# Turning taps and h2 on TensorE: 128-row transposes, or two of 64 rows in two banks of PSUM

## The chip, the cores and the metric

The kernel runs on one core of one Trainium2 chip (trn2). The metric is the device time of one execution in microseconds; the median of several runs is compared. All of the arithmetic is in 32-bit floats.

## The reference, cut to what matters

The input x has 4 images, 256 channels and 64 x 64 pixels. Two layers follow each other. The first works out, for each pixel, 49 attention weights (a 7 x 7 window with dilation 2) and sums the shifted inputs with them. The second is a bottleneck block with batch norms whose statistics come from the data.

```python
# layer 0
k = conv(x, w1 (128,256,7,7), pad 6, rhs_dilation 2) + b1
k = conv1x1(k, w2 (49,128)) + b2
attn = softmax(k, axis=1)                       # 49 weights for each pixel
x = einsum('bkchw,bkhw->bchw', shifts, attn)    # 49 shifted copies of x
# layer 1
residual = x
h = relu(bn(conv1x1(x, w1 (64,256))))
h = relu(bn(conv3x3(h, w2 (64,64))))
h = bn(conv1x1(h, w3 (256,64)))
return relu(h + residual)
```

`bn` is a batch norm over images and pixels: it takes mean and variance of its input, and applies gamma and beta.

## The kernel before, in words

One function, `conv_seq_kernel`, holds all stages. The stages follow each other in time like this.

**Logits (0 to about 475 us).** The two convolutions of layer 0 are merged into one of 49 outputs, and computed with a transform of the rows at nine points. `column_convs` (L251, its matmul is L262) multiplies column by column of the transformed input by the transformed weights and accumulates the 49 logits of the 4 strips of columns (s = 0 to 3), two accumulators each, in the eight banks of PSUM (`accall`, a tile of 8 banks). VectorE does the transforms and combinations, all through `stt` (L151).

**Softmax and the attention matrix.** The logits of a pixel lie along the free dimension, with pixels (rows of the image, blocks of images) on the partitions. `exponents(s)` (L520) subtracts the maximum and takes the exponential on ScalarE (L527), `shares(s)` (L529) divides by the sum and puts the 7 x 7 taps with gaps into one of three row buffers `pads` (L540), so that a window of 128 columns, at the right offset, is a diagonal band. `turn(s, h)` (L555) transposes those windows on TensorE (L566), which gives the band matrices that the gather needs. For each of the four row phases j it makes 8 transposes of 128 x 128 (two windows k, four columns w) into one pair of banks of `accall`; four pairs are used in rotation, by the counter `n_turn`. The only exception is turn(0, 0), which uses the first pair for all its j. The lower 64 of the 128 partitions hold images 0 and 2 (g = 0), the upper 64 hold images 1 and 3 (g = 1). So two copies bring each group into `amat`: g = 0 and g = 1. ScalarE makes both (L573), but where `shared` is set, VectorE makes that of g = 1 (L571). turn(0, 0) runs within the last column products, in an order that the framework's scheduler chooses. The seven others (L679 to L695) stand in a block where the order of VectorE, TensorE, ScalarE and SyncE is the order of the code: (0,1), (1,0), (1,1), (2,0), and then with `shared` (2,1), (3,0), (3,1). `zero_edges` (L651, its memset is L657) clears border blocks of `amat` on GpSimd.

**Gather and first 1x1 convolution (about 504 to 655 us).** `gather` (L739, matmul L752) multiplies tiles of x, pixels by channels, by blocks of `amat`. It takes all strips of columns of one image, so it needs all turns, the g = 0 half of them for the first units. The tiles of x come by DMA (`load_xt`, L113 to L119) and their shifted copies from `shift_xt` (L123 ScalarE, L124 and L125 GpSimd). `conv1` (L777, matmul L785) follows for every second unit. `keep_y` stores the result of layer 0, which is also the residual.

**3x3 convolution (about 660 to 717 us).** `direct` (L952) and `products` (L964) work in 8 single banks of a pool `pb`, and leave h2: 128 partitions (two halves of an image, a = 0 and 1, of 64 channels each), 16 blocks of 512 pixels.

**Statistics of the last convolution (about 720 to 742 us).** The moments of the third convolution follow from the second moments of h2. For each of the 16 blocks: ScalarE applies the batch norm and relu (L1024), TensorE transposes four times 128 x 128 into one bank (L1027), VectorE copies the bank into one of three buffers `ht` (L1029), in which a column of ones stands behind every 64 values, and TensorE accumulates 64 x 65 moments (L1032), for the two halves in the two column halves of the array. A float matmul takes two passes, which the trace shows as two records: 8 calls a block are 16 matmuls and 16 weight loads. A transpose is one record of each. The framework's scheduler orders this stage. `pt` comes from the pool of 8 banks, in which `moments` holds one.

**Last convolution and output (about 742 to 790 us).** `conv3` (L1009, matmul L1014) multiplies 64 rows of h2 by w3, alternately on the lower and upper 64 partitions; VectorE adds the residual (L1071), ScalarE applies the relu (L1076), SyncE stores.

Of the kernel before, what the change touches and what calls it, by code (L numbers as in the profile page):

```python
# [42 lines left out]
F32 = mybir.dt.float32  # L43
# [3 lines left out]
PSUM = bass.MemoryType.PSUM  # L47

P = 128
# [6 lines left out]
MID = 64  # L56
# [11 lines left out]
NS, WS = 4, 8  # L68
# [25 lines left out]
def conv_seq_kernel(ctx: ExitStack, tc: tile.TileContext, xp, xt, w1, b1, w2t, b2, m1t, g1, be1,  # L94
                    m2t, g2, be2, m3t, g3, be3, z, mask, pavg, out, ydram):
    nc = tc.nc
    def pool(stack, name, bufs, space=None, **kw):
        if space is not None:
            kw["space"] = space
        return stack.enter_context(tc.tile_pool(name=name, bufs=bufs, **kw))  # L100
# [143 lines left out]
    accall = pool(s_acc, "accp", 1, PSUM).tile([P, 2 * NS, 512], F32, name="acc")  # L244
# [243 lines left out]
    ident = late.tile([P, P], F32, name="ident")  # L488
# [8 lines left out]
    for g in range(2):  # L497
        half = slice(g * MID, (g + 1) * MID)
# [7 lines left out]
    outer = pool(ctx, "outerp", 1).tile([P, OUTER], F32, name="outer")  # L506
# [46 lines left out]
    n_turn = [0]  # L553

    def turn(s, h, shared=False):  # L555

        row = pads[(2 * s + h) % 3]
        for j in range(4):
            pt = accall[:, 2 * (n_turn[0] % NS) : 2 * (n_turn[0] % NS) + 2].rearrange("p a (m n) -> p (a m) n", n=P)
            if h == 0 and s == 0:  # L560
                pt = accall[:, :2].rearrange("p a (m n) -> p (a m) n", n=P)
            n_turn[0] += 1
            for k in range(2):
                for w in range(4):
                    o = 35 - (WS * s + 4 * h + w) + P * k
                    nc.tensor.transpose(pt[:, 4 * k + w, :], row[:, j, w, o : o + P], ident)  # L566
            for g in range(2):
                dst = amat[:, g, 2 * (2 * s + h) + j % 2, j // 2].rearrange("p (n k) e -> p k n e", k=2)
                src = pt[:, :, 64 * g : 64 * g + 64].rearrange("p (k w) n -> p k n w", k=2)
                if shared and g:  # L570
                    nc.vector.tensor_copy(dst, src)  # L571
                else:
                    nc.scalar.copy(dst, src)  # L573
# [49 lines left out]
    for n, (p, factor, left) in enumerate(passes):  # L623
        if n == 0:
            continue
        u = weights(n, 1)
        if p is None:
            for s in range(NS):
                visit(slots, strip(s), p, left)
            for t in pads:  # L630
                nc.gpsimd.memset(t, 0.0)
        for s in range(NS):
            if n == 2:
                apply_factor(slots, factor, NR - 2, strip(s))
            if p is not None:
                visit(slots, strip(s), p, left)
            for d in ([s] if s == 0 else []) + ([s + 1] if s + 1 < NS else []):
                put_back(n, d)
            column_convs(s, u, False)
            if p is None:  # L640
                for d in range(s - 1 if s else 0, s + 1 if s == NS - 1 else s):
                    last_outputs(d)
            elif s > 1:
                outputs(n, p, s - 2)
            if p is None and 0 < s < NS - 1:
                if s == 2:
                    turn(0, 0)
                exponents(s - 1)
                shares(s - 1)
# [12 lines left out]
    o = 4 * XT  # L662
# [3 lines left out]
    o = OUTER - NH1  # L666
# [9 lines left out]
    with tc.manual_schedule(  # L676
        engines={mybir.EngineType.DVE, mybir.EngineType.PE, mybir.EngineType.Activation, mybir.EngineType.SP}
    ):
        turn(0, 1)  # L679
        zero_edges(0)  # L680
        load_xt(xtiles[0], *units[0])
        exponents(2)
        turn(1, 0)
        exponents(3)
        shares(2)
        turn(1, 1)
        zero_edges(1)
        turn(2, 0)
        shares(3)
        load_xt(xtiles[1], *units[0], 1)  # L690
        turn(2, 1, True)
        zero_edges(2)
        turn(3, 0, True)
        turn(3, 1, True)
        zero_edges(3)  # L695
        xts[(*units[0], 0)], xts[(*units[0], 1)] = xtiles[:2]
        nc.scalar.preload_act_table(AF.Sqrt)
        more_xt(1)

    o = NH1  # L700
# [3 lines left out]
    o = 7 * C * 4  # L704
# [182 lines left out]

    sc1, sh1 = from_stats(st1, bn12[:, 0:1], bn12[:, 1:2], bank(0)[:, :3])
    s_acc.close()
    pb_ = pool(ctx, "pb", 8, PSUM)  # L890

# [102 lines left out]
    o = 4 * 2048  # L996

    HT = 8 * (MID + 1)
    ht = [outer[:, o + HT * i : o + HT * (i + 1)].rearrange("p (j g c) -> p j g c", j=4, g=2) for i in range(3)]
    o += 3 * HT  # L1000
    for t in ht:
        nc.gpsimd.memset(t[:, :, :, MID:], 1.0)
# [14 lines left out]
        return pt[:, :n]  # L1017


    moments = pb_.tile([P, 512], F32, tag="pb", name="moments")  # L1020
    blocks = [(slot, i, q) for slot in range(2) for i in range(2) for q in range(Q)]
    for n, (slot, i, q) in enumerate(blocks):
        v = h2[:, slot, q, 512 * i : 512 * (i + 1)]
        nc.scalar.activation(v, v, AF.Relu, bias=sh2, scale=sc2)  # L1024
        pt = pb_.tile([P, 512], F32, tag="pb", name="pturn2")
        for j in range(4):
            nc.tensor.transpose(pt[:, j * P : (j + 1) * P], v[:, j * P : (j + 1) * P], ident)  # L1027
        t = ht[n % 3]
        nc.vector.tensor_copy(t[:, :, :, :MID], pt.rearrange("p (j g c) -> p j g c", j=4, g=2))  # L1029
        for j in range(4):  # L1030
            for g in range(2):
                nc.tensor.matmul(  # L1032
                    moments[g * MID : (g + 1) * MID, : MID + 1],
                    t[:, j, g, :MID],
                    t[:, j, g, :],
                    start=(n == 0 and j == 0),
                    stop=(n == len(blocks) - 1 and j == 3),
                    skip_group_check=True,
                )
# [9 lines left out]
    pt = pb_.tile([P, 512], F32, tag="pb", name="pprod")  # L1049
# [3 lines left out]
    for half in range(NH):  # L1053
        c = slice(half * P, (half + 1) * P)
# [9 lines left out]
    for k, (b, i, half) in enumerate(blocks):  # L1064
        o = ops[k % 4]

        n = 256 if k in (0, len(blocks) - 1) else 512
        for lo in range(0, 512, n):
            for q in (0, 2, 1, 3):
                v = ys[b, q, i][:, half, lo : lo + n]  # L1070
# [65 lines left out]
```

## Time and profile before

| | |
|---|---|
| Runs (us) | 796.89, 794.95, 792.17; median 794.95 |
| Profiled execution (us) | 796.58 |
| Its span (us) | 794.3 |
| Mean granted clock of TensorE | 0.972 |
| L566, 256 transposes | first 463.5, last 503.6; 273 ns each from start to end |
| L573, ScalarE's 52 copies | first 464.6, last 503.9; 680 ns median |
| L571, VectorE's 12 copies | first 496.0, last 504.6; 692 ns median |
| L1027, 64 transposes | first 721.0, last 739.5 |
| L1029, 16 copies | first 722.1, last 740.2; 682 ns median |
| L1032, 256 matmuls of the moments | first 722.9, last 741.4; 222 ns median |

How to read the profile: the span is the time from the first instruction to the last, and the execution's own time is a little more than that. Times of single instructions run from start to end; instructions of one engine overlap, so the distance between starts, not the duration, tells how fast they follow each other. PE is TensorE's matmuls, PEld its weight loads, DVE is VectorE, ACT is ScalarE, POOL is GpSimd, SP is SyncE. In a line of the timeline the columns are: start, length of the merged piece, engine, line, operation, output and input with shapes, number of instructions, and in brackets the idle time ahead of it with what ended it. A shape like 128*128 in a matmul's line is rows by columns of the array that it uses. The chain is followed back from the last instruction: at each step to what released it, or to the instruction before it on its engine.

### The profile page before, as it was taken

The numbers are of one execution on the slowest core, as the hardware profiler recorded it, in microseconds if no ns is written. First come the engines' busy times: TensorE is split into PE (matmuls) and PEld (weight loads), VectorE is DVE, ScalarE is ACT, GpSimd is POOL, SyncE is SP. The second block draws the span as 40 slices with busy tenths as digits, with TensorE's granted clock in tenths as the row PEclk, the third lists the DMA queues.
The fourth block names the chain that finished last, engine by engine and source line by source line (L and its number), as shares of the span: only waits on it lengthen the run. The fifth ranks groups of instructions, "written<-read, shape, count | busy, mean of one in ns | idle before, by whom it ended". The sixth has DMA issues, their size and how long they took to land.

```text
span 794.3 us, 10929 instructions
## 1 busy us (share of the span) xinstructions
PE 725.6 (91%) x4208; PEld 585.4 (74%) x4208; DVE 574.2 (72%) x681; ACT 297.7 (37%) x594; POOL 75.3 (9%) x143
## 2 busy tenths in 40 slices
PE   0949998999999999996999999999999997996996
PEld 0838986888888888885888888988877873445642
DVE  4489989999466999899999966522232237574797
ACT  4640156111562201110101139534443437246497
POOL 3210010000000020000001202322222210000000
PEclk9979998999999999998999999999999998998998
DMA  7941089922789788220111012467776649442299
GB/s 282 381 165 41 0 281 287 376 87 94 254 298 395 242 344 305 72 62 10 51 32 42 3 57 64 144 234 227 234 253 216 221 170 386 171 145 95 82 394 371
DMA packets 59237, 150.26 MB, mean 189 GB/s; under 512 B 7346, under 2 KB 35634, under 8 KB 55090
## 3 DMA queue, kind: packets, MB, share of 16 engines
q1 hardware_dynamic: 51216, 141.11, 49.9%
q10 hardware_dynamic: 7970, 8.45, 3.0%
q8 instruction: 33, 0.54, 0.3%
q14 instruction: 18, 0.15, 0.1%
HBM read 93.81 MB, written 55.74 MB: 188 GB/s over the span
## 4 chain that ended last, share of the span: by engine, by line
PE 71%; DVE 16%; DMA 5%; ACT 4%; issue 2%; POOL 0%; SPq 0%; ACTq 0%; DVEq 0%; POOLq 0%
PE acc L262 42%; PE acc L752 12%; DVE arena L151 8%; DVE arena L1071 4%; PE acc L785 4%; PE pconv L964 3%; PE pdirect L952 3%; DMA outer<-in_xt_dram 2%; PE acc L566 2%; PE acc L325 2%; DMA w1raw<-in_w_dram 1%; PE pturn L1027 1%; ACT arena L573 1%; PE moments L1032 1%; DMA raw<-in_xp_dram 1%
## 5 line engine op out<-in xcount | busy, mean ns | idle before, releaser
L262 PE MATMUL acc<-arena 128*128 128x343 f32 (+3 forms) x2000 | 383.9, 355 | 20.7 <-DVE arena L151 20.7
L262 PEld LDWEIGHTS acc<-arena 128*128 128x128 f32 x2000 | 324.0, 193 | 79.5 <-issue 17.8
L151 DVE SCALAR_TENSOR_TENSOR arena<-arena 128x1024 f32<-128x1024 f32 (+7 forms) x192 | 290.4, 1558 | 27.8 <-PE acc L262 17.3
L752 PEld LDWEIGHTS acc<-arena,outer 128*128 128x128 f32 x1024 | 115.5, 192 | 11.4 <-issue 9.5
L752 PE MATMUL acc<-arena,outer 128*128 128x128 f32 x1024 | 118.1, 276 | 3.2 <-issue 2.2
L793 DVE BATCH_NORM_STATS2 st<-acc 128x6 f32<-128x512 f32 x16 | 11.2, 699 | 66.6 <-PE acc L785 66.4
L286 ACT COPY sv<-acc 128x392 f32<-128x392 f32 x40 | 19.1, 484 | 101.7 <-PE acc L262 93.9
L170 ACT COPY stage<-raw 128x128 f32<-128x128 f32 x128 | 43.5, 415 | 24.4 <-DMA raw<-in_xp_dram 24.0
L325 PE MATMUL acc<-powers,w1raw 128*128 128x196 f32 (+1 forms) x196 | 45.7, 397 | 6.9 <-DMA w1raw<-in_w_dram 5.6
L325 PEld LDWEIGHTS acc<-powers,w1raw 128*128 128x128 f32 x196 | 44.8, 315 | 7.5 <-DVE arena L151 5.7
L590 ACT COPY outer<-acc 128x784 f32<-128x784 f32 x8 | 6.5, 812 | 102.7 <-PE acc L262 83.3
L1014 PE MATMUL pconv<-arena,w3m 64*128 64x512 f32 (+1 forms) x144 | 42.8, 586 | 0.6 <-DVE arena L1071 0.6
L123 ACT COPY outer<-outer 64x2048 f32<-64x2048 f32 x15 | 28.4, 1895 | 36.8 <-DMA outer<-in_xt_dram 36.7
L151 DVE SCALAR_TENSOR_TENSOR outer<-outer 128x784 f32<-128x784 f32 (+2 forms) x47 | 36.9, 838 | 3.6 <-ACT outer L906 3.6
L1014 PEld LDWEIGHTS pconv<-arena,w3m 64*128 64x128 f32 x144 | 20.7, 185 | 21.9 <-DVE arena L1071 16.1
L773 DVE COPY bks<-acc 128x256 f32<-128x256 f32 x32 | 11.3, 417 | 33.8 <-PE acc L752 33.8
L1076 ACT ACTIVATE outer<-arena 128x512 f32<-128x512 f32 (+1 forms) x58 | 34.7, 695 | 1.3 <-DVE arena L849 1.1
L1071 DVE SCALAR_TENSOR_TENSOR arena<-pconv,arena 128x512 f32<-128x512 f32 (+1 forms) x58 | 34.3, 670 | 0.0
L124 POOL COPY outer<-outer 64x1792 f32<-64x1792 f32 x15 | 25.1, 1675 | 92.8 <-DMA outer<-in_xt_dram 79.8
L607 ACT COPY acc<-bks 128x392 f32<-128x392 f32 x40 | 18.5, 488 | 40.6 <-DVE outer L592 33.8
L573 ACT COPY arena<-acc 128x512 f32<-128x512 f32 x52 | 27.1, 716 | 14.8 <-PE acc L566 14.4
L964 PE MATMUL pconv<-outer,arena 128*128 128x512 f32 x72 | 31.1, 592 | 0.0
(143 smaller groups left out, 611.2 us busy)
## 6 DMA issues: line engine op xcount, KB each, us to landing
raw<-in_xp_dram SPq DMA_DIRECT2D x36, 608.0 KB, 5.4
outer<-in_xt_dram SPq DMA_DIRECT2D x17, 896.0 KB, 6.1
out_dram<-outer SPq DMA_DIRECT2D x14, 1024.0 KB, 4.5
arena<-y_dram SPq DMA_DIRECT2D x25, 512.0 KB, 7.5
fsort_dram<-stage SPq DMA_DIRECT2D x2, 4864.0 KB, 14.8
arena<-fsort_dram SPq DMA_DIRECT2D x8, 1216.0 KB, 9.8
y_dram<-outer SPq DMA_DIRECT2D x16, 512.0 KB, 5.4
aside_dram<-sv ACTq DMA_DIRECT2D x40, 196.0 KB, 5.7
```

What stands on the lines that cost most here:

```text
L123: nc.scalar.copy(t[:MID], x[MID:])
L151: nc.vector.scalar_tensor_tensor(out, in0, scalar, in1, ALU.mult, ALU.add)
L170: (last if last and k + a == 2 else nc.scalar.copy)(d[:, k, :, PLACE[b], 2 * a : 2 * a + 2, i : i + count], raw[:, lo : lo + 4 * count - 3 ...
L262: nc.tensor.matmul(acc[i][d][:, o : o + (hi - lo) * K], xi[:, i, CW * w : CW * w + CW, :].rearrange("p x t -> p (x t)"), u[i][:, lo * K : ...
L325: nc.tensor.matmul(pw[:, o : o + n], w1raw[:, :, u * K7 + v], powers[:, u, :n], start=(u == 0), stop=(u == K7 - 1), skip_group_check=True,)
L573: nc.scalar.copy(dst, src)
L752: nc.tensor.matmul(dst[:, :: NT - 1] if edge else pts[c][:, o : o + 128], x[:, i, half * P : (half + 1) * P], amat[:, b % 2, :, c, blocks, ...
L785: nc.tensor.matmul(pt[a * MID : (a + 1) * MID, :], w1m[:, n, :], ys[a, n][:, 512 * i : 512 * i + 512], start=(n == 0), stop=(n == NH - 1), ...
L964: nc.tensor.matmul(m[k], wu[:, k, j, :], vs[k][:, g, j : j + R, :], start=(j == 0), stop=(j == 1))
L1014: nc.tensor.matmul(pt[:, :n], w3m[part, half * P : (half + 1) * P], h2[part, slot, q, lo : lo + n], start=True, stop=True)
L1071: nc.vector.scalar_tensor_tensor(v, conv3(b, q, i, half, lo, n), sc3[:, half : half + 1], v, ALU.mult, ALU.add)
L1076: nc.scalar.activation(dst, v.rearrange("p (r w) -> p r w", w=R), AF.Relu, bias=sh3[:, half : half + 1])
```

## The change

Every transpose of 128 x 128 becomes two, one of partitions 0 to 63 and one of partitions 64 to 127, each with the matching 64 x 64 part of the identity. Each gives 128 partitions of 64 columns. The two outputs of a pair go into different banks: the results of g = 0 into one bank, those of g = 1 into the next.

In `turn`, a group of 8 transposes becomes 16, alternately g = 0 and g = 1. The pair of banks is the same as before, but what was split by window (k = 0 in one bank, k = 1 in the other) is now split by pair of images (g). So each of the two copies reads one bank, where it read 64 columns of every block in both.

In the h2 stage, 4 transposes a block become 8. Their output is one tile `turned` of four banks, used as two pairs in rotation (n % 2), where before each block took one of the pool's 8 banks. The pool `pb` is closed ahead of the stage, and a pool `pb3` of 4 banks takes its place for `moments`, the small products after it and `conv3`. The order of the parts of an `ht` buffer changes from (j, g, c) to (g, j, c). VectorE's copy of a block reads 256 columns from each of two banks.

```diff
-            pt = accall[:, 2 * (n_turn[0] % NS) : 2 * (n_turn[0] % NS) + 2].rearrange("p a (m n) -> p (a m) n", n=P)
+
+            pt = accall[:, 2 * (n_turn[0] % NS) : 2 * (n_turn[0] % NS) + 2].rearrange("p g (m n) -> p g m n", n=64)
             if h == 0 and s == 0:
-                pt = accall[:, :2].rearrange("p a (m n) -> p (a m) n", n=P)
+                pt = accall[:, :2].rearrange("p g (m n) -> p g m n", n=64)
             n_turn[0] += 1
             for k in range(2):
                 for w in range(4):
                     o = 35 - (WS * s + 4 * h + w) + P * k
-                    nc.tensor.transpose(pt[:, 4 * k + w, :], row[:, j, w, o : o + P], ident)
+                    for g in range(2):
+                        half = slice(64 * g, 64 * g + 64)
+                        nc.tensor.transpose(pt[:, g, 4 * k + w, :], row[half, j, w, o : o + P], ident[half, half])
             for g in range(2):
                 dst = amat[:, g, 2 * (2 * s + h) + j % 2, j // 2].rearrange("p (n k) e -> p k n e", k=2)
-                src = pt[:, :, 64 * g : 64 * g + 64].rearrange("p (k w) n -> p k n w", k=2)
+                src = pt[:, g].rearrange("p (k w) n -> p k n w", k=2)
...
     s_acc.close()
-    pb_ = pool(ctx, "pb", 8, PSUM)
+    s_pb = ExitStack()
+    pb_ = pool(s_pb, "pb", 8, PSUM)
...
-    ht = [outer[:, o + HT * i : o + HT * (i + 1)].rearrange("p (j g c) -> p j g c", j=4, g=2) for i in range(3)]
+    ht = [outer[:, o + HT * i : o + HT * (i + 1)].rearrange("p (g j c) -> p g j c", j=4, g=2) for i in range(3)]
...
+    s_pb.close()
+    turned = pool(ctx, "pturn", 1, PSUM).tile([P, 2, 2, 512], F32, name="pturn2")
+    pb_ = pool(ctx, "pb3", 4, PSUM)
     moments = pb_.tile([P, 512], F32, tag="pb", name="moments")
     blocks = [(slot, i, q) for slot in range(2) for i in range(2) for q in range(Q)]
     for n, (slot, i, q) in enumerate(blocks):
         v = h2[:, slot, q, 512 * i : 512 * (i + 1)]
         nc.scalar.activation(v, v, AF.Relu, bias=sh2, scale=sc2)
-        pt = pb_.tile([P, 512], F32, tag="pb", name="pturn2")
+
+        pt = turned[:, n % 2]
         for j in range(4):
-            nc.tensor.transpose(pt[:, j * P : (j + 1) * P], v[:, j * P : (j + 1) * P], ident)
+            for g in range(2):
+                half = slice(g * MID, (g + 1) * MID)
+                nc.tensor.transpose(pt[:, g, j * MID : (j + 1) * MID], v[half, j * P : (j + 1) * P], ident[half, half])
         t = ht[n % 3]
-        nc.vector.tensor_copy(t[:, :, :, :MID], pt.rearrange("p (j g c) -> p j g c", j=4, g=2))
+        nc.vector.tensor_copy(t[:, :, :, :MID], pt[:, :, : 4 * MID].rearrange("p g (j c) -> p g j c", j=4))
         for j in range(4):
             for g in range(2):
                 nc.tensor.matmul(
                     moments[g * MID : (g + 1) * MID, : MID + 1],
-                    t[:, j, g, :MID],
-                    t[:, j, g, :],
+                    t[:, g, j, :MID],
+                    t[:, g, j, :],
```

## The prediction

> **What bounds the kernel now.** I read the page first, then the chain that ended last in order of time, then short stretches of the timeline around the two places that the change touches, and last the starts of single instructions there.
>
> ```profile
> PE 725.6 (91%) x4208; PEld 585.4 (74%) x4208; DVE 574.2 (72%) x681; ACT 297.7 (37%) x594; POOL 75.3 (9%) x143
> PE 71%; DVE 16%; DMA 5%; ACT 4%; issue 2%; POOL 0%; SPq 0%; ACTq 0%; DVEq 0%; POOLq 0%
> ```
>
> TensorE is busy for 91% of the span and is 71% of the chain. But the transposes are few: 256 of L566 and 64 of L1027, and what they are worth differs by stretch. The chain around the first:
>
> ```profile
> 471.84 3.97 PE acc L262 x18
> 475.81 0.89 PE acc L566 x8
> ...
> 478.63 2.10 ACT arena L573 x4
> 480.73 1.48 ACT outer L527 x2
> 482.21 3.91 ACT arena L573 x8
> ...
> 496.70 7.21 PE acc L566 x64
> 503.91 17.93 PE acc L752 x160
> ```
>
> Up to 476.7 TensorE sets the pace (column products L262, with the four groups of turn(0,0) between). From 476.7 to 494.96 it is ScalarE: 2 copies for each group of 8 transposes, 0.48 us apart, and the exponentials. TensorE is a full ring of four bank pairs ahead and waits. From 496.70 it is TensorE again: 64 transposes, 8 groups of 0.87 us, and then the gather at once. How a group goes there:
>
> ```profile
> 499.32 0.69 DVE L571 COPY arena<-acc 128x512 f32<-128x512 f32 x1 [0.18 <-ACT arena L573]
> 499.58 0.59 ACT L573 COPY arena<-acc 128x512 f32<-128x512 f32 x1 [0.29 <-PE acc L566]
> 500.20 0.69 DVE L571 COPY arena<-acc 128x512 f32<-128x512 f32 x1 [0.18 <-ACT arena L573]
> ```
>
> ScalarE waits for TensorE, then VectorE waits for ScalarE, since both copies read the same two banks. In the h2 stretch (720.95 to 741.60, 20.65 us):
>
> ```profile
> 729.81 0.69 PE L1032 MATMUL moments<-outer 128*64 128x65 f32 x16
> 730.43 0.33 PE L1027 MATMUL pturn<-ident,arena 128*128 128x128 f32 x1
> 730.69 1.15 PE L1032 MATMUL moments<-outer 128*64 128x65 f32 x32
> 731.77 1.42 PE L1027 MATMUL pturn<-ident,arena 128*128 128x128 f32 x11
> ```
>
> TensorE never rests here: the same four pieces come back every 3.31 us for three blocks, while VectorE (0.65 us a copy) and ScalarE (0.71 us a block) could go faster.
>
> **What the Trainium skill says.** (1) "TensorE: Matmul & The Clock Gate", Terms, has a transpose mode that is four times faster for FP32. The trace shows part of that, in the weight load:
>
> ```profile
> 742.50 0.30 PEld L1055 LDWEIGHTS pm<-arena,w3m 128*128 128x128 f32 x2 [0.39 <-issue]
> 731.77 0.20 PEld L1027 LDWEIGHTS pturn<-ident,arena 128*128 128x128 f32 x2
> ```
>
> Two ordinary loads of 128 columns lie 0.11 us apart (0.30 less 0.19 for one), two loads of transposes 0.06 (57 ns by their starts). A transpose nevertheless takes 109 ns, start to start. So not the load but the 128 columns of the identity set its pace. (2) The same page, Part 3, "What overlaps and what doesn't": a load runs beside matmuls in flight when the row group differs. The trace agrees, at the only matmuls of 64 rows:
>
> ```profile
> 742.82 0.30 PEld L1014 LDWEIGHTS pconv<-arena,w3m 64*128 64x128 f32 x4
> 742.82 0.70 PE L1014 MATMUL pconv<-arena,w3m 64*128 64x256 f32 x4
> ```
>
> Four loads take as long as two of 128 rows: they start in pairs 6 ns apart, and so do the matmuls. (3) "TensorEngine Tiling (Array Packing)", Key Properties: changing the tiling mode drains TensorE. The trace agrees and gives the price. Three blocks are 12 transposes of 109 ns (1.31) and 24 pairs of L1032 ((1.15-0.22)/16 = 58 ns a pair, 1.40); 3.31 less 2.71 leaves 0.60 us for two changes there and back, 0.30 each. (4) "PSUM — Partial Sum Buffer", on bank collisions: no two engines may use one bank and quadrant together. That is why L571 waits for L573 above; copies out of two different banks need not.
>
> **The change, part by part.**
>
> *The price of a pair of halves.* Each half loads 128 columns (57 ns) and streams 64. At half of 109, streaming is 54. With both tiles at work at once a pair costs 54 to 58; if they go one after the other, 114 (two loads). Nothing in the trace shows transposes in two row tiles; the nearest row is the pair of L1032, two column tiles with 65 columns, 58 ns. I take 58, and keep 114 as a rival. Eight pairs are then 0.46 us where eight transposes were 0.87.
>
> *turn(0,0), between column products.* The products use all rows, so every group now has a change of mode before and after: 0.15 before, and 0.20 after, where an ordinary load of 0.11 is laid open. That is 0.35 a group against 0.41 gained. Groups j=1 to 3 reuse banks 0 and 1, whose two copies end 0.48 us apart; the halves g=0 may be put ahead alone, then nothing is paired (16 x 57 ns = 0.91) and there may be two changes (0.70): +0.74 a group. Bounds for the turn: -0.2 to +2.2; I take **+0.8**. Behind it on TensorE stand the last column products, and then turn(0,1), for which ScalarE waits. The first group of turn(0,1) gives 0.41 less one change: **-0.25**.
>
> *ScalarE's stretch, 18.2 us.* The copies keep 512 elements and one innermost step (64 elements where it was 128): **0**. TensorE's gain lies beside them.
>
> *The three shared turns.* (2,1), (3,0) and (3,1) have 12 copies on each engine. VectorE no longer waits for ScalarE. Its four of (2,1) follow TensorE from 493.1, after the last shares (L540), and end by 496.6; later ones follow at 0.60 us each (0.598 to 0.607 where it ran without a stop at 496). TensorE's (3,0) then waits only for ScalarE's copy of (2,1), whose data is free 0.95 us after its start: 495.75 where it was 496.70. From there a group costs 0.46 (TensorE), 0.48 (ScalarE), 0.60 (VectorE) instead of 0.87. Followed group by group with the ring of four: TensorE on the second group of (3,1) at 498.1, its ScalarE copy from 499.0 to 499.8, and the gather, which needs the g=0 half of the first two groups for its first column, at 499.85; before, 503.71. Of these 3.86 us, 0.25 are counted already: **-3.6**. What is late next: POOL's edge memsets (L657) and the shift L124 ahead of them. The load for L124 ends near 499 by the DMA's busy slices; 1.7 + 0.4 us of shift and some ten memsets bring the g=0 edges to about 503.1, and the edge matmuls come 28 x 113 ns after the start, at 503.0. It just fits; without that cover, up to 2.5 us come back. The gather itself is TensorE's, with 3.2 us of idling in 150, so an earlier start carries to its end.
>
> *h2.* Four transposes of a block, 0.44, become 0.23. But pturn2 has two buffers now, not seven: the transposes of block n+2 wait for the copy of block n, and behind that wait on TensorE stand the moments of n+1. I expect transposes and moments by turns, one change there and back a block: 0.23 + 0.47 + 0.30 = 1.00, where 1.10 was paid. The copy (0.05 + 0.68 + 0.08) hides behind the moments and the next transposes (about 1.1 with the changes). With M0 from 722.2 (now 722.94, with TensorE waiting for VectorE), half a microsecond lost to the lower clock at the start, and 15 blocks, the end is about 738.5, not 741.6: **-3.0** (-3.7 where the order keeps bigger groups).
>
> *Free edits.* The new ht order keeps each matmul's 64 and 65 elements in one run. The copy of 512 elements reads two banks instead of one. pools: the products' banks are empty by the time that from_sums has run. In the last stage four banks rotate where there were eight: a product of L1014 takes 1.12 us from start to end, VectorE needs it 3 x 0.66 = 1.98 after its bank came free. Hidden; if not, 50 steps would pay the difference.
>
> Sum: +0.8 - 0.25 - 3.6 - 3.0 = **-6.05 us**. The profiled execution took 796.58 (span 794.3 and 2.3 around it), so 790.5. It lies 1.6 above the median of the runs (794.95); the forecast is for the median: **788.9**.
>
> **Rivals.**
> *A, the forecast:* 788.9; 785.5 to 792.
> *B, the halves don't overlap* (the change doesn't do what it says): 114 ns a pair. Shared turns 0.91 a group, -0.6; h2 0.46 + 0.47 + 0.30 = 1.23 a block, +0.13 x 16 - 0.5 = +1.6; turn(0,0) +1.5. About +2.5: 797.4. For it: no transpose in row tiles in this trace. Against: L1014's loads and matmuls.
> *C, slower:* with two buffers TensorE's order in h2, which no hand wrote, becomes transposes and moments of the same block, as block 0 has it now. Then the copy is open each time: 0.24 + 0.22 + 0.81 + 0.47 + 0.10 = 1.85 a block, 29.6 for 20.65, +8.9, less 3.1 elsewhere: 800.8. It decides from (20.65 + 3.1)/16 = 1.48 us a block. Against: the order of now runs up to three blocks ahead.
> *D, the earlier gather is lost* to POOL or to loads: 2.5 of 3.6 come back, 791.4.
>
> **How the numbers follow.** A 0.60, D 0.16, B 0.12, C 0.12. Half a per cent, about what a measurement of this kernel can tell from no change, is 4 us: bounds 791.0 and 798.9. A gives faster but for its upper end (0.55), D with under half (0.07); same 0.05 + 0.09 + 0.10 = 0.24; slower C and the rest of B, 0.14. The range leaves out C and the tail of A: 785.5 to 797.5.
>
> **What would show it.** L1027 and L566 with 64*128, starts in pairs some 6 ns apart, pairs 58 ns apart (114: B). L571 no longer waiting for L573, and L752 beginning near 500. h2: the moments at an even 1.00 us, with VectorE waiting for TensorE (1.85 with TensorE waiting for VectorE: C). L1071 without idle time. If L262 between 463 and 476 stretches by more than 2 us, the step for turn(0,0) was wrong.

## The result, and the profile after

The changed kernel takes **817.83 us** (median of 6 runs, 816.11 to 820.47) where the kernel before takes 795.92 (6 runs, 792.17 to 799.19). The ratio is 1.0286, with a 95% interval of 1.0258 to 1.0315. It is slower by 2.9%, where 0.8% faster was forecast. The profiled execution of the changed kernel took 818.36 us, with a span of 815.8.

The page of the changed kernel:

```profile
PE 731.8 (90%) x4528; PEld 587.2 (72%) x4528; DVE 575.1 (70%) x681; ACT 297.4 (36%) x594; POOL 75.5 (9%) x143
...
PEclk9969999999999999989999989999999989955699
...
PE 60%; DVE 21%; DMA 10%; ACT 5%; issue 3%; POOL 0%; SPq 0%; ACTq 0%; DVEq 0%; POOLq 0%
```

The 320 new matmuls are there (4528 for 4208). Yet the busy time of TensorE went up by 6.2 us, and its share of the chain went down from 71% to 60%. The row of clocks says where to look: each digit is a fortieth of the span, in tenths of full speed. Before, no digit of the last ten was under 8; now "5 5 6" stands near the end, which is the h2 stretch and what follows.

A table by stages, read from the starts and ends of single instructions in both traces (us):

| stage | before | after | change |
|---|---|---|---|
| turn(0,0): first transpose to the end of L262 | 12.33 | 12.22 | -0.1 |
| end of L262 to the start of the gather (L752, now L755) | 27.94 | 24.83 | **-3.1** |
| h2: first transpose to the last moment | 20.65 | 41.04 | **+20.4** |
| last moment to the first residual add (L1071, now L1081) | 4.08 | 5.78 | +1.7 |
| first residual add to the last | 43.29 | 44.92 | +1.6 |

These five make 20.5 of the 21.5 us between the spans. The rest lies in stages whose code is the same, and they differ as much between executions: the gather to the end of the first 1x1 convolution is 150.8 in the profile of before, but 153.7 and 152.9 in two kernels below that keep its `turn`.

**The turn went nearly as priced.** The chain of the changed kernel just ahead of the gather, and its timeline there:

```profile
495.94 2.53 ACT arena L576 x4
498.51 18.13 PE acc L755 x160
```

```profile
493.68 4.18 PE L569 MATMUL acc<-ident,outer 64*128 64x64 f32 x127
493.94 5.47 DVE L574 COPY arena<-acc 128x512 f32<-128x512 f32 x9 [0.29 <-PE acc L569]
```

64 transposes took 7.21 us before; 127 halves now take 4.18. The halves of a pair start 10 ns apart, and pairs follow each other at 62 to 63 ns (58 was taken, 114 was rival B). Nine VectorE copies run one after the other, waiting for TensorE and no longer for ScalarE. The gather now waits for ScalarE's copies, L576, and begins at 498.51. In the stretch from L262 to the gather TensorE's mean granted clock is lower than it was (0.86, where it was 1.00 before). The stretch doesn't follow it: in `hand_order`, below, the clock there is 0.79 and the length 24.83 us as well.

**h2 did not.** The chain of the changed kernel there, and the sums of its waits from 717 to 759 (us in total, times, longest):

```profile
720.56 0.64 PE pturn L1037 x8
721.22 0.70 DVE outer L1039
722.06 1.14 PE moments L1042 x16
```

```profile
DVE outer L1039 <- PE pturn L1037: 29.7, 16, 1.9
PE moments L1042 <- DVE outer L1039: 12.8, 16, 0.9
```

Transposes, copy and moments follow each other in every one of the 16 blocks, none of them beside another, at about 2.54 us a block. TensorE waits for VectorE 16 times, and VectorE for TensorE 16 times. In the h2 stretch of before, VectorE waited for transposes 7 times, and TensorE for the copy once.

The mean granted clock shows the second half of it. The columns are the stretch, its length, the busy time of PE, PEld, DVE, ACT and POOL, the clock, the DMA's share and GB/s. First the changed kernel's h2 stretch and the gap behind it, then the h2 stretch of before:

```profile
716.90:758.90 42.00, 28.19 (x384) 23.28 (x384) 11.11 (x17) 11.39 (x16) 0.00 (x0) 0.50 0.06 21
758.90:764.70 5.80, 5.47 (x19) 3.80 (x18) 1.61 (x10) 0.29 (x1) 0.00 (x0) 0.50 0.01 3
```

```profile
720.90:741.65 20.75, 19.78 (x320) 17.19 (x320) 10.22 (x16) 10.59 (x15) 0.00 (x0) 0.87 0.08 27
```

TensorE is busy for 28.19 of 42.00 us, and its clock is 0.50 throughout. So the 16 moments of a block take 1.14 us in place of the 0.69 that the timeline of before showed. Both kernels enter h2 at half clock, since TensorE rests just ahead of it (3.59 us until VectorE's L868 and 2.46 until ScalarE's L1031 in this trace). The Trainium skill ("TensorE: Matmul & The Clock Gate", Part 1: The HAM clock gate) lets the clock fall to half after an idle window of about 3.4 us. This trace agrees: the clock fell at 716.2, after 4.8 us in which TensorE was busy for 0.41. Before, it was back at 1.00 from 726.2, which is 5.2 us into h2; here it is back only from 770.8, in the output stage.

### The profile page after: what moved, and what is told of

It reads as the page before. It is cut to its first block, busy times and chain, and to the rows that moved or that the text cites. A ratio compares the mean times of both kernels' runs of the same rounds, so it can differ in the third digit from the quotient of the medians.

```text
span 815.8 us, 11563 instructions
## 1 busy us (share of the span) xinstructions
PE 731.8 (90%) x4528; PEld 587.2 (72%) x4528; DVE 575.1 (70%) x681; ACT 297.4 (36%) x594; POOL 75.5 (9%) x143
## 4 chain that ended last, share of the span: by engine, by line
PE 60%; DVE 21%; DMA 10%; ACT 5%; issue 3%; POOL 0%; SPq 0%; ACTq 0%; DVEq 0%; POOLq 0%
PE acc L262 32%; PE acc L755 11%; DVE arena L151 9%; PE acc L788 4%; DVE arena L1081 3%; PE pconv L968 3%; PE pdirect L956 3%; DMA outer<-in_xt_dram 2%; ACT arena L576 2%; PE moments L1042 2%; PE acc L325 2%; DMA fsort_dram<-stage 2%; DVE stage_x L151 2%; DVE outer L1039 1%; PE pturn L1037 1%
## 5 line engine op out<-in xcount | busy, mean ns | idle before, releaser
L262 PE MATMUL acc<-arena 128*128 128x343 f32 (+3 forms) x2000 | 382.5, 354 | 20.9 <-DVE arena L151 20.5
L262 PEld LDWEIGHTS acc<-arena 128*128 128x128 f32 x2000 | 322.7, 192 | 79.6 <-issue 16.5
L755 PEld LDWEIGHTS acc<-arena,outer 128*128 128x128 f32 x1024 | 115.5, 192 | 14.3 <-issue 12.8
L755 PE MATMUL acc<-arena,outer 128*128 128x128 f32 x1024 | 118.1, 276 | 6.0 <-issue 2.8
L1018 PE MATMUL pconv<-arena,w3m 64*128 64x512 f32 (+1 forms) x144 | 46.4, 645 | 0.5 <-DVE arena L1081 0.5
L1018 PEld LDWEIGHTS pconv<-arena,w3m 64*128 64x128 f32 x144 | 23.4, 208 | 22.4 <-DVE arena L1081 16.5
L1081 DVE SCALAR_TENSOR_TENSOR arena<-pconv,arena 128x512 f32<-128x512 f32 (+1 forms) x58 | 34.7, 665 | 1.2 <-PE pconv L1018 1.1
L1039 DVE COPY outer<-pturn 128x512 f32<-128x512 f32 x16 | 11.1, 691 | 29.7 <-PE pturn L1037 29.7
```

The costliest lines, as they stand in the source:

```text
L262: nc.tensor.matmul(acc[i][d][:, o : o + (hi - lo) * K], xi[:, i, CW * w : CW * w + CW, :].rearrange("p x t -> p (x t)"), u[i][:, lo * K : ...
L755: nc.tensor.matmul(dst[:, :: NT - 1] if edge else pts[c][:, o : o + 128], x[:, i, half * P : (half + 1) * P], amat[:, b % 2, :, c, blocks, ...
L1018: nc.tensor.matmul(pt[:, :n], w3m[part, half * P : (half + 1) * P], h2[part, slot, q, lo : lo + n], start=True, stop=True)
L1081: nc.vector.scalar_tensor_tensor(v, conv3(b, q, i, half, lo, n), sc3[:, half : half + 1], v, ALU.mult, ALU.add)
```

## Experiments

The first theory after the result was rival C: TensorE's **order** became transposes and moments of the same block, so the copy is open each time. Its rival was that the **halves** themselves cost more in h2 than in the turn. Two kernels split the change, and a third gave TensorE the other order.

**The turn alone** (`turn_only`): the kernel before, with only the part of the diff in `turn`.

```diff
...
-                    nc.tensor.transpose(pt[:, 4 * k + w, :], row[:, j, w, o : o + P], ident)
+                    for g in range(2):
+                        half = slice(64 * g, 64 * g + 64)
+                        nc.tensor.transpose(pt[:, g, 4 * k + w, :], row[half, j, w, o : o + P], ident[half, half])
...
```

> The kernel before with the change to turn alone; h2 as before. Order theory (the loss comes from TensorE's order in the h2 stretch and the low clock that follows from it) and halves theory (halves in row tiles, with two pairs of banks, are slow by themselves in h2) agree that the turns gain: pairs of halves 62 ns apart, the gather 5.2 us earlier, of which the changed kernel's trace kept 3.0 at the end of the first 1x1 convolution. About 793, ratio 0.996. The h2 stretch 20.7 us as before.

Measured: 793.27 us for 795.88, ratio 0.9956 (0.9935 to 0.9977). Its stages are 12.22 and 24.84, as in the full change, and h2 takes 20.89. So the turn is a gain of about 2.6 us.

**h2 alone** (`h2_only`): the kernel before, with all other parts of the diff.

```diff
...
-        pt = pb_.tile([P, 512], F32, tag="pb", name="pturn2")
+        pt = turned[:, n % 2]
...
-            nc.tensor.transpose(pt[:, j * P : (j + 1) * P], v[:, j * P : (j + 1) * P], ident)
+            for g in range(2):
+                half = slice(g * MID, (g + 1) * MID)
+                nc.tensor.transpose(pt[:, g, j * MID : (j + 1) * MID], v[half, j * P : (j + 1) * P], ident[half, half])
...
```

> The kernel before with the change to the h2 stretch and its banks alone; turn as before. Both theories: h2 stretch 41 us instead of 20.7, the way from the last moment to the first L1081-like step 5.8 instead of 4.1, the output stage 44.9 instead of 43.3: +23.7, about 819.5. If it is below 815, part of the loss needs both changes together.

Measured: 818.14 us, ratio 1.0280 (1.0244 to 1.0316); h2 takes 41.10, the gap 5.78, the output stage 44.91. The loss is here. The two parts, -2.6 and +22.3, sum to +19.7 where the whole change measured +21.9; the interval of this run, 2.9 us to each side, covers the difference.

**The order by hand** (`hand_order`): the full change, with the loop body cut into `turn2` (relu and transposes) and `moments2` (copy and moments). The transposes of the next block go ahead of the moments of this one.

```diff
...
+    with tc.manual_schedule(engines={mybir.EngineType.PE}):
+        for n in range(len(blocks) + 1):
+            if n < len(blocks):
+                turn2(n)
+            if n >= 1:
+                moments2(n - 1)
...
```

> The changed kernel with TensorE's order in h2 written out: transposes of block n+1 ahead of the moments of block n. Same halves, same two pairs of banks in one tile. Order theory: 1.00 us a block, full clock, h2 stretch 17.7 us, TensorE not waiting for VectorE after the first block; about 790, ratio 0.993. Halves theory: still over 1.6 us a block, over 803.

Measured: 816.94 us, ratio 1.0242 (1.0204 to 1.0281), 2.55 us a block. **The order theory fell**: TensorE's order is the wanted one, and the time is nearly the same. The number fits the halves theory, but the timeline doesn't:

```profile
722.11 1.13 PE L1049 MATMUL moments<-outer 128*64 128x65 f32 x16 [0.88 <-DVE outer L1046]
723.17 0.69 PE L1040 MATMUL pturn<-ident,arena 64*128 64x64 f32 x8
723.90 0.69 DVE L1046 COPY outer<-pturn 128x512 f32<-128x512 f32 x1 [1.94 <-PE pturn L1040]
```

The transposes at 723.17 belong to block n+1. VectorE, which has been idle for 1.94 us, should have copied block n while the moments ran; its transposes were long done. It begins only after those of block n+1. So it is in the whole stretch: the copies of the first 15 blocks each start 0.04 to 0.05 us after the end of the next block's transposes, and 0.75 (the first) to 2.67 us after the end of their own. `turned` is **one tile** with two slices. If the two aren't told apart, this is what one would see. That gave a new theory, one tile, with the half clock as its amplifier.

**Two tiles** (`two_tiles`): the full change, but the pool hands out a tile for each block; the order is again the framework's.

```diff
-    turned = pool(ctx, "pturn", 1, PSUM).tile([P, 2, 2, 512], F32, name="pturn2")
+    turned = pool(ctx, "pturn", 2, PSUM)
...
-        pt = turned[:, n % 2]
+        pt = turned.tile([P, 2, 512], F32, tag="pturn", name="pturn2")
```

> The changed kernel with the two pairs of banks as two tiles of a pool that rotates, instead of two slices of one tile; no order by hand. Order theory: the scheduler lets the transposes run up to two blocks ahead, with two changes of mode there and back for two blocks, so 1.0 to 1.1 us a block, h2 stretch 18 to 19 us, about 791, ratio 0.994. Halves theory: no difference to the changed kernel, 818.

Measured: 797.8 us, ratio 1.0023 (1.0010 to 1.0036). h2 falls from 41.04 to 23.78. The same PSUM, the same instructions and the same halves, so 17.3 us hung on how the two pairs of banks were declared. It still isn't a gain: the clock is 0.50 for the first 9.1 us of h2, and then two blocks take 2.63. The order is 14 halves, 16 moments, 2 halves and 16 moments:

```profile
733.51 0.65 PE L1037 MATMUL pturn<-ident,arena 64*128 64x64 f32 x14
735.32 0.27 PE L1037 MATMUL pturn<-ident,arena 64*128 64x64 f32 x2
```

The next 14 start at 736.14. The copies of both blocks lie behind the 14, and TensorE waits 0.54 us for the first of them.

**Whole transposes in one tile** (`full_one_tile`): the kernel before with its own `turn` and no halves at all; only the tile with two slices is taken from the change, with the new pools and the new order of `ht` that go with it.

```diff
...
-        pt = pb_.tile([P, 512], F32, tag="pb", name="pturn2")
+        pt = turned[:, n % 2, 0]
...
```

> The kernel before (turn too), but h2's four transposes of 128 by 128 write into one bank of either slice of the one tile of four banks; the new pools and the new order of ht as in the changed kernel. No halves at all. One-tile theory (two slices of one tile tie the transposes of a block to the copy of the one before, and force the order): order by turns, half clock, about 2.9 us a block (four transposes at half clock 0.87 where eight halves are 0.43), h2 stretch 46, about 824. Halves theory: the stretch goes back to 20 to 23 us, about 797.

Measured: 827.01 us, ratio 1.0371 (1.0334 to 1.0408), h2 47.81, and in its timeline

```profile
732.26 1.12 PE L1032 MATMUL pturn<-ident,arena 128*128 128x128 f32 x4
733.41 0.69 DVE L1034 COPY outer<-pturn 128x512 f32<-128x512 f32 x1 [2.37 <-PE pturn L1032]
734.16 1.14 PE L1037 MATMUL moments<-outer 128*64 128x65 f32 x16 [0.79 <-DVE outer L1034]
```

The same chain stands here without a single half, at 2.97 us a block. The halves theory is excluded: with one tile they save 0.43 us a block (2.97 less 2.54).

**The clock apart from the order** (`filler`): the full change with its one tile; behind the transposes of each block TensorE gets four matmuls more that nobody reads. TensorE's order is that of the changed kernel, written out by hand.

```diff
...
+        for _ in range(4):
+            nc.tensor.matmul(spare_bank[:, :P], ident, ident, start=True, stop=True, skip_group_check=True)
...
```

> The changed kernel with four products of the identity with itself, into a spare bank that nobody reads, after the transposes of each block; TensorE's order in h2 otherwise as the changed kernel has it (written out). It isolates the clock: the copy stays open in each block. If the half clock is a result of TensorE's idling and adds to the loss: after some 9 us full clock, 1.9 to 2.1 us a block instead of 2.54, h2 stretch 33 to 35 instead of 41, 4.1 us instead of 5.8 behind it; about 808 in all. If the clock has another cause or no part in it: 818 or above, since work was added.

Measured: 808.83 us, ratio 1.0150 (1.0119 to 1.0180), h2 36.03. Its timeline and its window from 728:

```profile
730.54 0.46 PE L1041 MATMUL pturn<-ident,arena 64*128 64x64 f32 x8
732.02 0.69 PE L1052 MATMUL moments<-outer 128*64 128x65 f32 x16
```

```profile
728.00:745.00 17.00, 17.00 (x268) 14.95 (x268) 5.53 (x8) 0.00 (x0) 0.00 (x0) 1.00 0.01 2
```

With TensorE never at rest, the clock is 1.00 from 721.1, 5.5 us into h2; the halves of a block take 0.46 for the 0.69 of `hand_order` and its moments 0.69 for 1.14. A block takes 2.10 us, less than 2.54 in spite of the added 1.16. The gap behind h2 is 4.07 again, and the output stage, with the four banks, 43.43. So **adding work that nobody reads gained 9 us** against the changed kernel (817.83), though not against the kernel before.

**Two tiles and the order by hand** (`two_tiles_hand`): both edits from above together.

> The changed kernel with two rotating tiles, and TensorE's order written out: transposes of block n+1 ahead of the moments of block n. One-tile theory: now VectorE's copy of a block waits for that block's transposes alone; 1.00 us a block at full clock, as the forecast had it, some 1.7 while the clock is still low at the start; h2 stretch 18.5 to 20 us; output stage still 44.5 with four banks; about 792, ratio 0.995. If it stays over 2 us a block as hand_order did, the tie isn't by the tile.

Measured: 792.83 us, ratio 0.9949 (0.9926 to 0.9971), h2 18.78, and in its timeline

```profile
724.85 0.46 PE L1040 MATMUL pturn<-ident,arena 64*128 64x64 f32 x8
725.24 0.69 PE L1049 MATMUL moments<-outer 128*64 128x65 f32 x16
725.35 0.69 DVE L1046 COPY outer<-pturn 128x512 f32<-128x512 f32 x1 [0.32 <-PE pturn L1040]
```

The copy starts 0.11 us after the moments of the block ahead of it and runs wholly beside them. Moments start every 1.01 us (723.22, 724.23, 725.24), which is the 1.00 of the forecast.

**Two blocks at a time** (`batch_8`): the order by hand again, with three tiles of two banks, the transposes of two blocks and then the moments of two, and eight banks for the last convolution again.

```diff
...
-    turned = pool(ctx, "pturn", 1, PSUM).tile([P, 2, 2, 512], F32, name="pturn2")
...
+    turned = pool(s_st, "pturn", 3, PSUM)
...
+    with tc.manual_schedule(engines={mybir.EngineType.PE}):
+        turn2(0)
+        for k in range(0, len(blocks), 2):
+            for n in (k + 1, k + 2):
+                if n < len(blocks):
+                    turn2(n)
+            for n in (k, k + 1):
+                moments2(n)
...
+    s_st.close()
+    pb_ = pool(ctx, "pb4", 8, PSUM)
```

> An attempt at a faster version: three rotating pairs of banks in h2, TensorE's order written out in groups of two blocks (transposes of two, moments of two), and eight banks again for the last convolution. 0.92 us a block at full clock, h2 stretch 17.5 to 19; output stage 43.3 where four banks gave 44.5 to 44.9; with the turns' 3.1 us about 789.5, ratio 0.992.

Measured: 791.32 us (788.35 to 794.14), ratio 0.9929 (0.9897 to 0.9961); h2 17.71. This version is faster than both kernels: 5.6 us (0.7%) under before.

**Whose gain is it, the halves' or the hand order's** (`full_batch`): `batch_8`, with whole transposes in h2 again.

```diff
...
-            for g in range(2):
-                half = slice(g * MID, (g + 1) * MID)
-                nc.tensor.transpose(pt[:, g, j * MID : (j + 1) * MID], v[half, j * P : (j + 1) * P], ident[half, half])
+            nc.tensor.transpose(pt[:, 0, j * P : (j + 1) * P], v[:, j * P : (j + 1) * P], ident)
...
```

> batch_8 with one thing taken back: h2 is transposed in whole 128 by 128 squares again (64 transposes, each block into one bank of its pair), with the same three tiles, the same order by hand of two blocks and two blocks, and the halves in turn. If the halves are what makes the h2 stretch shorter, two blocks take 8 x 109 ns (0.87) for the transposes, 0.93 for the moments and 0.30 for the changes there and back, 2.10 us where batch_8 takes 1.87: the stretch is longer by 8 x 0.23 = 1.8 us, about 19.5 for 17.71, and the median about 793.1. If the order by hand alone shortened the stretch, it is 17.7 again.

Measured: 791.17 us, ratio 0.9937 (0.9912 to 0.9961). The medians of the two can't be told apart, but the stretch can: 19.47 us, and two blocks in 2.11. First `full_batch`, then `batch_8`:

```profile
724.15 1.09 PE L1039 MATMUL pturn<-ident,arena 128*128 128x128 f32 x8
726.26 1.09 PE L1039 MATMUL pturn<-ident,arena 128*128 128x128 f32 x8
```

```profile
725.81 0.71 PE L1041 MATMUL pturn<-ident,arena 64*128 64x64 f32 x16
727.68 0.71 PE L1041 MATMUL pturn<-ident,arena 64*128 64x64 f32 x16
```

The next transposes start 2.11 us on with whole ones and 1.87 with halves. Of the 2.9 us that h2 lost from before (20.65) to `batch_8` (17.71), 1.2 come with the order and the buffers and 1.8 with the halves. These are stretches of one execution each; the half clock at their start can't have made the second gain, since it lasted longer in `batch_8` (5.75 us of h2) than in `full_batch` (4.66). That the 1.8 us aren't seen in the medians is no contradiction, as they are 0.2% and the intervals are 0.2 to 0.3% to each side; but no median shows them either.

## Why the prediction was wrong

**The step that failed** is one sentence in h2: "But pturn2 has two buffers now". I read `turned[:, n % 2]` as two buffers. It is one tile, and its slices are tied: in `hand_order` the copy of a block waits until the next block's transposes, which go into the other slice, are done. So what was built on it fell as well: "I expect transposes and moments by turns" (the order was transposes and moments of the same block), and "The copy ... hides behind the moments and the next transposes" (it hid behind nothing). The forecast for h2 was -3.0; it came out at +20.4. `full_one_tile` shows it without halves, `two_tiles` and `two_tiles_hand` show that it goes when the tile is split. With the tile split, "by turns" still didn't come from the framework: in `two_tiles` a block takes 1.32 us at full clock, and the 1.00 of the forecast came only with the order by hand.

**Rival C** had the place and the wait, at a chance of 0.12, but not the cause: it laid the order to having only two buffers, and with two real ones (`two_tiles`) the order is another. Its price was too small as well: 1.85 us a block where 2.54 was measured, and 800.8 for 817.83. What the price lacked is the clock. An open copy lets TensorE rest in each block, and the clock, at half when h2 began, stayed there. Of the 0.69 us between 1.85 and 2.54, at least 0.44 are shown to be the clock's, by `filler` (2.54 less 2.10); the filler's own 1.16 us outlast the copy by about 0.2, since the copy ends at 731.74 and the moments begin at 732.02. Without that a block would take some 1.9 at full clock, by estimate, which is near C's 1.85. The 11.4 us of C that are missing in h2 (41.04 less 29.6), with 1.7 in the gap and 1.6 in the output stage, make 14.7 of the 17.0 between C and the result; 1.0 more is that the runs of before had a median of 795.92 this time, not 794.95. The last 1.3 are not traced.

**The price of a pair**, 58 ns, was right (62). Rival B is excluded: by these starts and by the gain of `turn_only`.

**turn(0,0)**, +0.8 within -0.2 to +2.2, came out at -0.1, near the lower bound. The +0.74 a group that were put down for halves ahead alone were not paid: but for a few at the edges of a group, the halves start in pairs. **The first group of turn(0,1) and the shared turns**, -3.85 together, came out at -3.1. The sum of the turn is -3.2 for -3.05, which is luck: errors of 0.9 and 0.75 cancel. ScalarE's copies set the last 2.5 us ahead of the gather, as the prediction's walk through the groups had it, though the gather began at 498.51 and not near 500: L262 ended 2.1 us earlier in this execution.

**Rival D**, the earlier gather lost again: no kernel here isolates it. Against it stands that the median of `turn_only` falls by 2.6 us, most of the 3.2 that its stages show, and that the stretch from the gather to the end of the first 1x1 convolution is no longer with the new `turn` (150.6 to 153.1 us in the profiles of eight kernels) than with the old (150.8 to 153.7 in three).

**The free edits.** Four banks for the last convolution are hidden, as forecast: 43.43 and 43.42 us in `filler` and `two_tiles_hand`, against 43.29 with eight. The 1.6 us that the output stage lost in the changed kernel goes with its clock, which is 0.50 until 770.8. `two_tiles` has 44.45 there, and its clock is 0.50 from 749.75 to 753.1 and 1.00 ahead of that and behind it; why it fell there stays open.

Open as well: the traces show that the two slices of `turned` are tied, not by which rule of the framework. It isn't so of every tile in slices. `acc` is one tile too, with its eight banks used as four pairs in rotation, and the lines of the turn above show that TensorE writes 127 halves into it in 4.18 us without a wait while copies read the pairs that it filled before. No kernel here tests what sets the two tiles apart.

## What to carry to other kernels

Don't count a slice of a tile as a buffer unseen: in this kernel the slices of `acc` served as buffers, those of `turned` didn't. Where two stages are to overlap, a tile for each turn is the safer form, and the trace tells whether the reader starts after its own writer or after the next one. Price an opened wait on TensorE at half clock as well as at full; here the difference was 0.44 us or more of each 2.54 us block, and 3.3 us behind it. A part that was priced well can sit beside one that wasn't: split the change before judging the idea, since with real buffers the stretches of both places were shorter with the halves.

## What was not expected of the hardware

TensorE was busy for 28.19 of 42.00 us, with no rest of over 1.0 us after its first transposes, and still had a clock of 0.50 for all of it. In `full_one_tile` it was busy for 35.00 of the 47.81 us of h2, and the clock was 0.50 too. With the gaps filled (`filler`) it was 0.50 for 5.5 us of h2 and then 1.00; in `two_tiles`, with fewer rests (busy for 8.35 of 9.11 us), it rose to 1.00 at 729.2. The Trainium skill ("TensorE: Matmul & The Clock Gate", A second HAM failure mode: psum-queue depth-cycling) tells of short rests between groups of matmuls that make the clock swing between half and full. Here it didn't swing, it stayed down for 54.5 us (716.3 to 770.8), which no figure of an idle window would have foretold from the rests of 0.8 to 0.9 us in h2.

How short the rests must be for the clock to rise isn't measured. The filler's matmuls also aren't transposes, so it could be asked whether the clock answers to the rests or to the kind of work. The kernel before speaks for the rests: its clock rose after the first 5.15 us of h2, in which transposes took 3.20 us and moments only 1.14.
